# Window attention in blocks of 64 tokens, eight heads at a time, on two column tiles

## The chip, the cores and the metric

The kernel runs on one core of a Trainium2 chip. The time is device microseconds of one execution; the kernel before has a median of 1505.85 us over three runs (1504.56 to 1506.03). One more execution was profiled: 1506.56 us, of which its span in the profile is 1504.9 us. All durations below are from that execution.

## The reference

The input x holds 16 sequences ("batches" below) of 512 tokens with 128 channels. Two sublayers follow each other, each with a residual: attention in a window, and then a product-key mixture of experts. Only the first is touched here:

```python
def attn(x, w_qkv, w_proj):              # x: layer-normalised, 16 x 512 x 128
    q, k, v = split(x @ w_qkv.T)         # 16 heads of 8 channels
    s = q @ k.T / sqrt(8)                # per head, 512 x 512
    s = where(abs(i - j) > 128, -1e9, s) # a band of 128 tokens to either side
    return (softmax(s) @ v).reshape(...) @ w_proj.T
x = x + attn(layernorm(x))
x = x + experts(layernorm(x))
```

The second sublayer normalises over the whole batch of tokens, so it starts when attention is done with all 16 sequences.

## The kernel before, in words

**Units.** Attention runs over units of four heads of one sequence: 16 sequences times 4 groups, 64 units. Each unit has four steps, one for each block of 128 tokens. One pass of the loop over `s` is one step; `divmod(s, NQ)` gives unit and block.

**Operands.** `prepare(b)` normalises a sequence, transposes it, multiplies it by the weights and cuts q and k into three bf16 pieces each (on POOL), so that a sum of bf16 products has fp32 accuracy. The pieces go to DRAM (`write`), and `lay(n)` brings those of one unit back into `qst` and `kst` with six DMAs, the pieces stacked on the partition axis; a seventh DMA zeroes the three rows of `qst` from row 96. There are six buffers of each. All these DMAs stand in the queue of SP.

**Two products of the same operands.** `greatest(n, t)` multiplies the queries of one block by the keys of its neighbours (256 keys in an outer block, 384 in an inner one), four heads, into `s_ps`. DVE adds the band mask and takes the greatest of each row in one instruction (line 424). When the unit's four steps are done, `greatest_pieces` cuts the negated maxima into three bf16 pieces (five POOL operations), and `greatest_rows` transposes them on PE (`mT_ps`), copies them on ACT and sends them by DMA into the three rows of `qst`, where the matching rows of `kst` are ones. So the second product, `exponentials(n, u)` into `e_ps` with keys as rows and queries as columns, comes out with the maxima subtracted; ACT takes the exponential into `pT` (line 466). POOL then sets what is outside the band to zero with `affine_select` (through the helper at line 172), one 128 x 128 block for each neighbour, for four heads in one instruction.

**Weighing.** `weigh(n, u)` multiplies the fp32 `pT` by the values: four heads at once, each on a column tile of 32 of TensorE, summed over the steps in one PSUM bank (`o_ps`). `vaug` holds the values and a column of ones, which gives the sum for the division. `divide` transposes a unit's result (`t_ps`) and divides on DVE; `project(b)` transposes and projects a whole sequence.

**Order.** PE, through `mm` and `tr`, and POOL, through `pool`, keep the order of the program. One step emits on PE: s, e, e, s, the o products of two steps earlier (`LATE`), s, e, e, s, and then at most one block that needs the one bank of `ps_m`: `mT_ps`, `t_ps`, or the next piece of `preparing`, `ending` or `beside`. The maxima run `AHEAD` = 2 units before the exponentials, and `lay` runs four units before, at block 2. Three PSUM banks each serve `s_ps` and `e_ps`.

Of the kernel before, what the change touches and what calls it, by code (L numbers as in the profile page):

```python
# [10 lines left out]
F32 = mybir.dt.float32  # L11
# [32 lines left out]
def kernel(  # L44
# [18 lines left out]
    NG = NH // 4  # L63
# [42 lines left out]
    band_f = const.tile([P, 3, P], F32, name="band_f")  # L106
    nc.gpsimd.memset(band_f, 0.0)
    for i, sign in ((0, 1), (2, -1)):
        nc.gpsimd.affine_select(
            out=band_f[:, i], in_=band_f[:, i], compare_op=ALU.is_ge, fill=-MASKED,  # L110
            base=0, pattern=[[sign, P]], channel_multiplier=-sign,
        )
    band = const.tile([P, 3, P], BF16, name="band")
# [39 lines left out]
    with ExitStack() as at:  # L153
# [3 lines left out]
        w3 = at.enter_context(tc.tile_pool(name="w3", bufs=3))  # L157
        dr = at.enter_context(tc.tile_pool(name="dr", bufs=2, space=bass.MemoryType.DRAM))
# [21 lines left out]
        tr(wt_ps[:, 3 * P :], w_proj_sb, ident)  # L180
        for c, w in enumerate((wqT, wkT, wvT, wprojT)):
            wt = wt_ps[:, c * P : (c + 1) * P]
            if c < 2:

                w, wt = w.rearrange("p (d h) -> p d h", d=DK), wt.rearrange("p (h d) -> p d h", d=DK)
            nc.vector.tensor_copy(w, wt)
# [67 lines left out]
        vaug = [fix.tile([P, NQ, NH, VW], F32, name=f"vaug_{i}") for i in range(3)]  # L254
# [5 lines left out]
        zeros = fix.tile([P, T], BF16, name="zeros")  # L260
        nc.gpsimd.memset(zeros, 0.0)

        masked = [fix.tile([P, 3 * P], BF16, name=f"masked_{i}") for i in range(4)]

        NU, NBUF = B * NG, 6
        qst = [fix.tile([P, 4, T], BF16, name=f"qst_{i}") for i in range(NBUF)]
        kst = [fix.tile([P, 4, T], BF16, name=f"kst_{i}") for i in range(NBUF)]
# [71 lines left out]
        def prepare(b):  # L339

            xnT = w2.tile([P, T], F32, tag="xnT", name=f"xnT_{b}")
# [32 lines left out]
            if b < 3:  # L374
                nc.gpsimd.memset(va, 0.0)
                nc.gpsimd.memset(va[:, :, :, DK : DK + 1], 1.0)
            v_ps = ps_m.tile([P, NQ, NH, DK], F32, tag="m", name=f"v_ps_{b}")
            for t in range(NQ):
                mm(
                    v_ps[:, t].rearrange("p h k -> p (h k)"),  # L380
                    lhsT=xnT[:, t * P : (t + 1) * P], rhs=wvT, start=True, stop=True,
                )
            nc.scalar.copy(va[:, :, :, 0:DK], v_ps)
# [4 lines left out]
        def lay(n):  # L388
# [4 lines left out]
            for what, st in (("q", qst[n % NBUF]), ("k", kst[n % NBUF])):  # L393
                src = pieced[what, b].rearrange("s (d h) t -> s d h t", d=DK)
                for i in range(3):
                    side = src[i if what == "q" else slice(0, 3)]
                    if what == "q":
                        side = bc(side, 0, 3)
                    nc.sync.dma_start(
                        st[3 * i * DK : 3 * i * DK + 3 * DK], side[:, :, 4 * g : 4 * g + 4]  # L400
                    )

            nc.sync.dma_start(qst[n % NBUF][NR : NR + 3], bc(zeros[0:3], 1, 4))

        def near(t):

            return [u for u in (t - 1, t, t + 1) if 0 <= u < NQ]

        def greatest(n, t):

            q, k = qst[n % NBUF], kst[n % NBUF]
            if t == 0:
                tops[n] = w2.tile([P, NQ, 4], F32, tag="mx", name=f"mx_{n}")
            us = near(t)
            k0, w = us[0] * P, len(us) * P
            from_u = P if t == 0 else 0
            for h in range(4):
                s_ps = ps_s.tile([P, 3, P], F32, tag="s", name=f"s_ps_{n}_{t}_{h}")
                s = s_ps.rearrange("p u k -> p (u k)")[:, 0:w]
                mm(  # L420
                    s, lhsT=q[:, h, t * P : (t + 1) * P], rhs=k[:, h, k0 : k0 + w],
                    start=True, stop=True,
                )
                nc.vector.tensor_tensor_reduce(  # L424
                    masked[h][:, 0:w], s, band.rearrange("p u k -> p (u k)")[:, from_u : from_u + w],
                    1.0, LOWEST, ALU.add, ALU.max, tops[n][:, t, h : h + 1],
                )
                yield

        def greatest_pieces(n):  # L430

            top = tops.pop(n)
            mp = w2.tile([P, NQ, 3, 4], BF16, tag="mp", name=f"mp_{n}")
            rest = w2.tile([P, NQ, 4], F32, tag="mr", name=f"mr_{n}")
            pool("tensor_scalar_mul", rest, top, -1.0)
            pool("tensor_copy", mp[:, :, 0], rest)
            pool("tensor_tensor", rest, rest, mp[:, :, 0], ALU.subtract)
            pool("tensor_copy", mp[:, :, 1], rest)
            pool("tensor_tensor", mp[:, :, 2], rest, mp[:, :, 1], ALU.subtract)
            tops[n] = mp  # L440

        def greatest_rows(n):

            mp = tops.pop(n)
            mT_ps = ps_m.tile([12, NQ, P], BF16, tag="m", name=f"mT_ps_{n}")
            for t in range(NQ):
                tr(mT_ps[:, t], mp[:, t].rearrange("p s h -> p (s h)"), ident_bf)
            mT = w2.tile([12, T], BF16, tag="mT", name=f"mT_{n}")
            nc.scalar.copy(mT, mT_ps.rearrange("r t q -> r (t q)"))
            for i in range(3):  # L450
                nc.sync.dma_start(qst[n % NBUF][NR + i : NR + i + 1], mT[4 * i : 4 * i + 4])

        def exponentials(n, u):
# [3 lines left out]
            ts = near(u)  # L457
            q0, w = ts[0] * P, len(ts) * P
# [613 lines left out]
```

## Time and profile before

| | |
|---|---|
| median of 3 runs | 1505.85 us |
| profiled execution | 1506.56 us, span 1504.9 us |
| first s product / first e product | 38.18 us / 53.25 us |
| last block of attention on PE (xi of the last sequence) | starts at 710.98 us |
| share of the span busy | PE 93%, DVE 87%, ACT 81%, POOL 73% |
| maxima (DVE, line 424) | 1024, 459.1 us busy, mean 484 ns |
| exponentials (ACT, line 466) | 1024, 389.4 us busy, mean 436 ns |
| selects (POOL, line 172) | 384, 239.2 us busy, mean 639 ns |
| s products / e products (PE) | 1024 / 1024, mean 307 ns / 302 ns |
| o products (PE) | 2048 passes, mean 447 ns |
| DMA | mean 50 GB/s over the span, 179 GB/s in the first 40 us |

Attention takes a little under the first half of the span. In the views, "busy" of PE is from the start of a product to a modelled end that includes its way through the array, so products that follow each other closely overlap; how fast PE really goes is read from the distance between starts. A group of instructions is named by line, engine, operation, output and inputs, with partitions x elements; "128\*64" means 128 rows and 64 columns of the array. An fp32 product appears as two passes.

### The profile page before, as it was taken

The numbers are of one execution on the slowest core, as the hardware profiler recorded it, in microseconds if no ns is written. First come the engines' busy times: TensorE is split into PE (matmuls) and PEld (weight loads), VectorE is DVE, ScalarE is ACT, GpSimd is POOL, SyncE is SP. The second block draws the span as 40 slices with busy tenths as digits, with TensorE's granted clock in tenths as the row PEclk, the third lists the DMA queues.
The fourth block names the chain that finished last, engine by engine and source line by source line (L and its number), as shares of the span: only waits on it lengthen the run. The fifth ranks groups of instructions, "written<-read, shape, count | busy, mean of one in ns | idle before, by whom it ended". The sixth has DMA issues, their size and how long they took to land.

```text
span 1504.9 us, 48591 instructions
## 1 busy us (share of the span) xinstructions
PE 1395.0 (93%) x16880; PEld 844.1 (56%) x16880; DVE 1315.6 (87%) x7999; ACT 1212.4 (81%) x2596; POOL 1094.5 (73%) x1706
## 2 busy tenths in 40 slices
PE   3999999999999999896789999999999999999997
PEld 1445555544545545443456666666666666666666
DVE  6878888878888887882899999999999999999984
ACT  1577777777777777775889999999999999999963
POOL 8466666777777767563577887788878788788775
PEclk9999999999999999997999999999999999999989
DMA  6233332223333222320000000000000000000000
GB/s 177 86 111 101 102 94 84 85 79 89 92 91 92 86 85 76 101 63 36 10 9 10 9 17 10 16 17 9 16 10 17 17 10 16 10 16 10 10 2 24
DMA packets 53574, 74.96 MB, mean 50 GB/s; under 512 B 5840, under 2 KB 39888, under 8 KB 53200
## 3 DMA queue, kind: packets, MB, share of 16 engines
q1 hardware_dynamic: 52496, 71.59, 16.2%
q8 instruction: 134, 2.20, 0.6%
q14 instruction: 112, 0.92, 0.2%
q10 hardware_dynamic: 832, 0.26, 0.1%
HBM read 49.28 MB, written 20.97 MB: 47 GB/s over the span
## 4 chain that ended last, share of the span: by engine, by line
DVE 47%; PE 3%; issue 1%; ACT 1%; POOL 0%; ACTq 0%; POOLq 0%
DVE idx L624 10%; DVE row L624 9%; DVE place L624 6%; DVE top L624 6%; DVE mine L624 5%; DVE best L624 4%; DVE x_ps L624 3%; DVE num L624 2%; DVE upper L624 1%; PE up_ps L624 1%; DVE zs L624 1%; PE w_ps L624 1%; POOL cols L624 0%; PE dn_ps L624 0%; PE off_ps L624 0%
## 5 line engine op out<-in xcount | busy, mean ns | idle before, releaser
L424 DVE CUSTOM_DVE_ANT_0 masked<-s_ps,band 128x384 bf16<-128x384 f32 (+1 forms) x1024 | 459.1, 484 | 112.2 <-PE s_ps L168 95.7
L466 ACT ACTIVATE pT<-e_ps 128x384 f32<-128x384 f32 (+1 forms) x1024 | 389.4, 436 | 117.5 <-PE e_ps L168 111.1
L172 POOL TENSOR_SCALAR_AFFINE_SELECT pT<-pT 128x512 f32<-128x512 f32 x384 | 239.2, 639 | 188.8 <-ACT pT L466 187.2
L168 PE MATMUL s_ps<-kst,qst 128*128 128x384 bf16 (+1 forms) x1024 | 309.5, 307 | 22.2 <-DMA kst<-kv 11.0
L624 POOL TENSOR_TENSOR cols<-mine,wT 64x512 f32<-64x512 bf16 x256 | 270.0, 1055 | 25.7 <-ACT row L624 7.0
L624 PE MATMUL w_ps<-cols,row 128*64 128x32 f32 x8192 | 260.0, 224 | 13.6 <-POOL cols L624 13.6
L624 PEld LDWEIGHTS w_ps<-cols,row 128*64 128x64 f32 x8192 | 252.1, 139 | 32.3 <-POOL cols L624 27.8
L168 PE MATMUL e_ps<-qst,kst 128*128 128x384 bf16 (+1 forms) x1024 | 228.7, 302 | 13.1 <-ACT pT L466 12.4
L624 POOL TENSOR_TENSOR g<-g,gel 128x512 f32<-128x512 f32 x128 | 163.6, 1278 | 105.5 <-ACT g L624 105.5
L168 PEld LDWEIGHTS <-qst 128*128 128x128 bf16 x1024 | 100.5, 98 | 196.2 <-issue 168.4
L168 PE MATMUL o_ps<-pT,vaug 128*32 128x384 f32 (+1 forms) x2048 | 192.3, 447 | 0.4 <-POOL pT L172 0.4
L624 DVE FIND_INDEX8 idx<-top,sim 128x8 uint32<-128x32 f32 x1024 | 166.2, 185 | 0.0
L624 ACT ACTIVATE row<-off_p,one 128x512 f32<-128x512 bf16 x256 | 165.8, 749 | 0.0
L624 ACT ACT_TABLE_LOAD x122 | 156.5, 1283 | 2.2
L624 DVE TENSOR_TENSOR row<-x_ps,nums_p 128x1024 f32<-128x1024 f32 x128 | 150.0, 1213 | 0.0
L624 PE MATMUL up_ps<-g,key_out_sb 64*128 64x256 f32 (+2 forms) x1152 | 148.0, 384 | 0.0
L624 ACT ACTIVATE off_p<-off_ps 128x512 bf16<-128x512 f32 x256 | 132.4, 602 | 17.0 <-PE off_ps L624 16.8
L624 PE MATMUL dn_ps<-xt,key_inT 128*64 128x256 f32 x1024 | 125.6, 388 | 2.2 <-ACT sim L624 1.4
L168 PEld LDWEIGHTS <-kst 128*128 128x128 bf16 x1024 | 99.9, 98 | 45.4 <-issue 23.9
L624 PE MATMUL off_ps<-p_bf,ident_bf 128*128 128x512 bf16 x256 | 96.6, 377 | 19.7 <-ACT p_bf L624 19.6
L624 PEld LDWEIGHTS dn_ps<-xt,key_inT 128*64 128x64 f32 x1024 | 68.3, 137 | 78.3 <-ACT row L624 41.7
L624 DVE MAX8 top<-sim 128x8 f32<-128x32 f32 x1024 | 106.7, 177 | 2.9 <-ACT sim L624 2.9
(145 smaller groups left out, 2366.5 us busy)
## 6 DMA issues: line engine op xcount, KB each, us to landing
qst<-qv SPq DMA_DIRECT2D x192, 96.0 KB
kst<-kv SPq DMA_DIRECT2D x192, 96.0 KB
qv<-qp SPq DMA_DIRECT2D x16, 384.0 KB
kv<-kp SPq DMA_DIRECT2D x16, 384.0 KB
x<-in_L_attn_x_dram SPq DMA_DIRECT2D x16, 256.0 KB
xT<-xiT SPq DMA_DIRECT2D x16, 256.0 KB
xt<-xT SPq DMA_DIRECT2D x16, 256.0 KB
out_dram<-o_sb SPq DMA_DIRECT2D x16, 256.0 KB
```

The source lines that it names most:

```text
L168: tc.keep_in_program_order(nc.tensor.matmul(*args, **kw))
L172: tc.keep_in_program_order(getattr(nc.gpsimd, op)(*args, **kw))
L424: nc.vector.tensor_tensor_reduce(masked[h][:, 0:w], s, band.rearrange("p u k -> p (u k)")[:, from_u : from_u + w], 1.0, LOWEST, ALU.add, A ...
L466: nc.scalar.activation(pT[:, h, 0:w], e_ps[:, 0:w], AF.Exp)
L624: return lambda *args, **kw: tc.keep_in_program_order(op(*args, **kw))
```

## The change

The 64 units of four heads become 32 of eight. A block is 64 tokens, so a unit has eight steps; a step still makes four maxima and four exponentials, each now for a pair of heads `r` and `4 + r`: one head's 64 tokens lie on partitions 0 to 63, the other's on 64 to 127, each from its own product on a column tile of 64. A block sees two blocks of 64 to either side, so the products have 192, 256 or 320 columns. What lies outside the band are now corners of 64 x 64, selected for each half of the partitions by itself: two or four instructions a step.

The maxima of eight heads are transposed in one go (96 rows) and reach `qst` in two DMAs. `weigh` takes 128 rows that hold two heads: `vaug` has the first head's values in columns 0 to 15 of the upper partitions and the second's in columns 16 to 31 of the lower ones, so that one column tile of 32 makes both. The order of the heads changes with it, which the weights `wqT`, `wkT` and `wprojT` absorb at the start. v is computed on column tiles of 64 and copied in two halves. `qst` and `kst` have four buffers of twice the size; the zero rows are copied from unused rows of the same tile; `xnT`, `oT` and `aT` have one buffer in place of two. The maxima run 13 steps before the exponentials (8 before), and `lay` runs 20 steps before.

```diff
-    NG = NH // 4
+    HB = P // 2
+    NS = T // HB
+    NG = NH // 8
+    NR4 = 4
...
-    for i, sign in ((0, 1), (2, -1)):
+    for v in range(2):
+        half = band_f[v * HB : v * HB + HB]
         nc.gpsimd.affine_select(
-            out=band_f[:, i], in_=band_f[:, i], compare_op=ALU.is_ge, fill=-MASKED,
-            base=0, pattern=[[sign, P]], channel_multiplier=-sign,
+            out=half, in_=half, compare_op=ALU.is_ge, fill=-MASKED,
+            base=0, pattern=[[1, 5 * HB]], channel_multiplier=-1,
         )
...
+        w1 = at.enter_context(tc.tile_pool(name="w1", bufs=1))
...
-        tr(wt_ps[:, 3 * P :], w_proj_sb, ident)
+        w_proj_of = const.tile([P, NH // 2, 2, DK], F32, name="w_proj_of")
+        for j in range(2):
+            nc.vector.tensor_copy(
+                w_proj_of[:, :, j], w_proj_sb.rearrange("p (j a d) -> p j a d", j=2, d=DK)[:, j]
+            )
+        tr(wt_ps[:, 3 * P :], w_proj_of.rearrange("p a j d -> p (a j d)"), ident)
...
+                for g in range(NG):
+                    for j in range(2):
+                        nc.vector.tensor_copy(w[:, g, j], wt[:, g, j])
...
-        NU, NBUF = B * NG, 6
-        qst = [fix.tile([P, 4, T], BF16, name=f"qst_{i}") for i in range(NBUF)]
+        NU, NBUF = B * NG, 4
+        qst = [fix.tile([P, 8, T], BF16, name=f"qst_{i}") for i in range(NBUF)]
...
-            v_ps = ps_m.tile([P, NQ, NH, DK], F32, tag="m", name=f"v_ps_{b}")
-            for t in range(NQ):
-                mm(
-                    v_ps[:, t].rearrange("p h k -> p (h k)"),
-                    lhsT=xnT[:, t * P : (t + 1) * P], rhs=wvT, start=True, stop=True,
+            v_ps = ps_m.tile([P, NS, HB], F32, tag="m", name=f"v_ps_{b}")
+            for i in range(NS):
+                for j in range(2):
+                    mm(
+                        v_ps[j * HB : j * HB + HB, i], lhsT=xnT[:, i * HB : i * HB + HB],
+                        rhs=wvT[:, j * HB : j * HB + HB], start=True, stop=True, skip_group_check=True,
+                    )
+            for j in range(2):
+                half = slice(j * HB, j * HB + HB)
+                nc.scalar.copy(
+                    va[half, :, :, 16 * j : 16 * j + DK],
+                    v_ps[half].rearrange("p c (a k) -> p c a k", k=DK),
                 )
-            nc.scalar.copy(va[:, :, :, 0:DK], v_ps)
...
-            nc.sync.dma_start(qst[n % NBUF][NR : NR + 3], bc(zeros[0:3], 1, 4))
+            nc.sync.dma_start(qst[n % NBUF][NR : NR + 3], qst[n % NBUF][NR - 4 : NR - 1])
...
+        def greatest(n, i, r):
...
+            us = near(i)
+            k0, w = us[0] * HB, len(us) * HB
+            from_u = (us[0] - i + 2) * HB
+            s_ps = ps_s.tile([P, T], F32, tag="s", name=f"s_ps_{n}_{i}_{r}")
+            for j in range(2):
+                h = NR4 * j + r
                 mm(
-                    s, lhsT=q[:, h, t * P : (t + 1) * P], rhs=k[:, h, k0 : k0 + w],
-                    start=True, stop=True,
+                    s_ps[j * HB : j * HB + HB, 0:w], lhsT=q[:, h, i * HB : i * HB + HB],
+                    rhs=k[:, h, k0 : k0 + w], start=True, stop=True, skip_group_check=True,
                 )
...
+            rows = 3 * NR4 * NS
+            mT_ps = ps_m.tile([rows, P], BF16, tag="m", name=f"mT_ps_{n}")
+            tr(mT_ps, mp.rearrange("p s r i -> p (s r i)"), ident_bf)
+            mT = w2.tile([rows, P], BF16, tag="mT", name=f"mT_{n}")
+            nc.scalar.copy(mT, mT_ps)
+            for j in range(2):
+                nc.sync.dma_start(
+                    qst[n % NBUF][NR : NR + 3, NR4 * j : NR4 * j + NR4], mT[:, j * HB : j * HB + HB]
                 )
...
+            for j in range(2):
+                h = NR4 * j + r
                 mm(
-                    e_ps[:, 0:w], lhsT=k[:, h, u * P : (u + 1) * P], rhs=q[:, h, q0 : q0 + w],
-                    start=True, stop=True,
+                    e_ps[j * HB : j * HB + HB, 0:w], lhsT=k[:, h, i * HB : i * HB + HB],
+                    rhs=q[:, h, q0 : q0 + w], start=True, stop=True, skip_group_check=True,
                 )
...
+        def outside_band(n, i):
+
+            us = near(i)
+            for u, sign in ((i - 2, 1), (i + 2, -1)):
+                if u in us:
+                    at = (u - us[0]) * HB
+                    for j in range(2):
+                        side = probs[n, i][j * HB : j * HB + HB, :, at : at + HB]
+                        pool(
+                            "affine_select", out=side, in_=side, compare_op=ALU.is_ge, fill=0.0, base=0,
+                            pattern=[[0, NR4], [sign, HB]], channel_multiplier=-sign,
+                        )
...
-            for j in range(4):
+            for r in range(NR4):
                 mm(
-                    outs[n][32 * j : 32 * j + 32, q0 : q0 + w], lhsT=vaug[b % 3][:, u, 4 * g + j],
-                    rhs=pT[:, j, 0:w], start=u == 0, stop=u == NQ - 1, skip_group_check=True,
+                    outs[n][VW * r : VW * r + VW, q0 : q0 + w], lhsT=vaug[b % 3][:, i, NR4 * g + r],
+                    rhs=pT[:, r, 0:w], start=i == 0, stop=i == NS - 1, skip_group_check=True,
                 )
...
-        AHEAD, LAID, LATE = 2, 4, 2
+        AHEAD, LAID, LATE = 13, 20, 2
...
-            next(tops_of, None)
-            next(probs_of, None)
-            next(tops_of, None)
-            if 0 <= s - LATE < NU * NQ:
-                weigh(*divmod(s - LATE, NQ))
-            together(tops_of, probs_of)
+            for r in range(NR4):
+                steps = [(greatest, s + AHEAD, r), (exponentials, s, r)]
+                for what, at_s, r in steps if r % 2 == 0 else steps[::-1]:
+                    if 0 <= at_s < NU * NS:
+                        what(*divmod(at_s, NS), r)
+                if r == 1 and 0 <= s - LATE < NU * NS:
+                    weigh(*divmod(s - LATE, NS))
+            if 0 <= s < NU * NS:
+                outside_band(n, u)
             free = True
-            if u == 0 and 0 <= n + AHEAD - 1 < NU:
-                greatest_pieces(n + AHEAD - 1)
-            if u == 1 and 0 <= n + AHEAD - 1 < NU:
-                greatest_rows(n + AHEAD - 1)
+            m, of = divmod(s + AHEAD, NS)
+            if of == 0 and 0 < m <= NU:
+                greatest_pieces(m - 1)
+            if of == 1 and 0 < m <= NU:
+                greatest_rows(m - 1)
                 free = False
```

## The prediction

> **What bounds the kernel now.** I first read the page's 40 slices and then the windows. Attention fills the first half, up to about 700 us; the expert half after it is the same code in both kernels. The windows (columns: busy time and count of PE, weight loads, DVE, ACT, POOL, then granted clock, DMA share, GB/s) give the steady stretch of attention:
>
> ```profile
> 200.00:400.00 200.00, 194.19 (x1606) 100.56 (x1608) 163.42 (x738) 153.76 (x392) 140.87 (x275) 0.99 0.29 86
> 400.00:600.00 200.00, 192.36 (x1594) 98.27 (x1595) 167.23 (x746) 153.92 (x392) 143.12 (x278) 1.00 0.30 88
> ```
>
> A busy PE need not be a full one, so next I read the timeline of PE alone. The reader should see the starts: each product starts when the one before has streamed, not when it ends.
>
> ```profile
> 508.19 0.34 PE L168 MATMUL s_ps<-kst,qst 128*128 128x384 bf16 x1
> 508.36 0.49 PE L168 MATMUL e_ps<-qst,kst 128*128 128x384 bf16 x2
> 508.69 0.33 PE L168 MATMUL s_ps<-kst,qst 128*128 128x384 bf16 x1
> 508.94 0.64 PE L168 MATMUL o_ps<-pT,vaug 128*32 128x256 f32 x8
> 509.51 0.34 PE L168 MATMUL s_ps<-kst,qst 128*128 128x384 bf16 x1
> ```
>
> A 384-wide product takes 0.163 us (508.69 is three after 508.19, with 0.17 first), that is 384 columns at 2.4 per ns plus 3 ns. The eight 256-wide o passes start 0.25 after the last s (0.16 of it streaming, 0.09 a gap) and hold PE 0.57: 4 x 256/2.4 = 0.427, four column tiles side by side, plus 0.143. So a change from 128 columns to 32 and back costs 0.09 + 0.145 = 0.235 us.
>
> Sum for one batch (4 groups of 4 steps, widths 256, 384, 384, 256): s and e 4 x 8 x 1280/2.4 = 17.1, plus 3 ns x 128 = 0.4; o 4 x 4 x 1280/2.4 = 8.5; 16 changes 3.8; four mT blocks at 0.42 (517.53 to 517.86 and the gap before) 1.7; four t_ps at 0.43 1.7; xn 0.43, q and k 0.86 each, v 0.9, a 0.43, y 0.9, xi 0.43, together 4.8. That is 38.0 us. The stretch holds 638 maxima (64 a batch), so a batch lasts 400 x 64/638 = 40.1. What PE waits for is in the tile view of mp:
>
> ```profile
> who waited for it (us, times):
>   PEld L175: 14.5, 36
>   PE mT_ps L175: 2.4, 7
> ```
>
> 16.9 us in ten batches is 1.7 a batch; 0.4 is left. PE bounds attention, and the other engines need 33.1 (DVE), 30.8 (ACT) and 28.5 (POOL) of the 40.1.
>
> **The change, part by part, per batch** (now two groups of eight steps, widths 192, 256, 4 x 320, 256, 192: 2176 a group).
>
> *s and e.* 128 products become 128 pairs on two column tiles. Whether a pair costs one stream or two decides everything. The expert half has such pairs:
>
> ```profile
> 899.48 0.59 PE L624 MATMUL sim_ps<-wsim,xb 128*128 128x512 f32 x1
> 900.00 1.95 PE L624 MATMUL dn_ps<-xt,key_inT 128*64 128x256 f32 x16
> 906.74 0.28 PE L624 MATMUL x_ps<-ident_bf,num_bf 128*64 128x64 bf16 x6
> 908.88 0.38 PE L624 MATMUL off_ps<-less_nums,ident_bf 128*128 128x512 bf16 x1
> 909.19 0.34 PE L624 MATMUL s_ps<-ident,share 128*64 128x64 f32 x4
> 909.45 1.13 PE L624 MATMUL up_ps<-g,key_out_sb 64*128 64x256 f32 x8
> ```
>
> Sixteen dn passes of 256 fp32 columns (0.213 each by the 2 cycles a column seen in q_ps) end in 1.95: seven spacings plus one of 0.379 makes 0.22 a pair, so a pair costs one stream and its weight loads hide. Six bf16 products end in 0.28 although one takes 0.196. So a pair is width/2.4 + 3 ns: 2 x 8 x 2176/2.4 = 14.5 + 0.4. Bounds: one stream, or two (+14.5 us a batch, 1704 in all); I take one, because dn is the same tile shape.
>
> The Trainium skill, TensorEngine Tiling (Array Packing), Restrictions, says that column tiling disables the fast weight load; its page TensorE: Matmul & The Clock Gate, LDWEIGHTS, gives columns/1.2 ns. By an estimate from that, two loads of 64 take 107 ns, which exceeds only the 192-wide stream of 80: 27 ns x 32 pairs, 0.9 us a batch, 14 us in all, 1486 for 1472. No run here shows that; the x_ps row speaks against it.
>
> *o.* 4 x 2176/2.4 x 2 = 7.25; still one change per step, 3.8.
>
> *mT and t_ps.* Four transposes into one of 96 columns; half as many blocks: 2 x 0.053 and 2 x 0.43.
>
> *New changes of tiling.* s and e now stand at 64 columns, so each 128-column block (mT 2, t_ps 2, xn, q, k, a, y, xi: 10) pays a change in and out. Priced by the rows above: sim 128 to dn 64 leaves 0.52 - 0.427 = 0.09; off to s_ps 0.31 - 0.213 = 0.09; s_ps to up_ps 0.26 - 0.107 = 0.15. Again 0.235: 2.35 a batch. Bounds 0 and twice that (1434 and 1510); I take the rows. v_ps moves into the 64 mode: 16 pair passes at the 0.062 of w_ps (128 products in 3.96), 1.0 for 0.9. Other blocks unchanged, 3.9.
>
> PE sum: 14.9 + 7.25 + 3.8 + 0.1 + 0.86 + 2.35 + 1.0 + 3.9 = 34.1.
>
> *Selects on POOL.* 24 of 128x512 become 48 of 64x256.
>
> ```profile
> L172 POOL TENSOR_SCALAR_AFFINE_SELECT pT<-pT 128x512 f32<-128x512 f32 x89 | 55.6, 641 | 45.4 <-ACT pT L466 45.2
> L109 POOL TENSOR_SCALAR_AFFINE_SELECT band_f<-band_f 128x128 f32<-128x128 f32 x2 | 0.5, 294 | 0.0
> ```
>
> Between 128 and 512 elements the slope is 0.9 ns, so 256 take 0.41, or 0.385 in a row (0.27 and 0.615 for the two shapes). Half the partitions save nothing: four 64-partition cols products in a row take 4.42 (1.1 each), not side by side. Bounds 0.2 (side by side) and 0.64. 18.5 for 15.
>
> *Pieces.* Five POOL operations per group, 1.39 from first to last, twice instead of four times. POOL in all: 28.5 - 15 - 4.4 + 18.5 + 2.5 = 30.
>
> *Where the stall goes.* mT waits on PE for the pieces, and everything behind it on PE waits too. Before, the pieces followed a step with one select (0.64). Now they come at u == 3, behind four. The selects start 0.8 after the step's last s (510.01 to 510.99 less streaming), take 1.56, the pieces 1.45: ready at 3.8. PE reaches mT one 320-wide step later (8 x 0.136 + 0.533 + 0.235 = 1.86) plus 0.09, in even groups also after a_ps (0.67): stalls of 1.8 and 1.2, 3.0 a batch for 1.7. W (the o products) two steps on finds its selects done; where POOL carries 0.6 to 1.2 of query and key pieces per step it still keeps up (9.8 us against PE's 10.2 over the four wide steps).
>
> *DVE, ACT.* The maxima cost 0.345 at 256 and 0.478 at 384 in a row, so 0.28 and 0.41 at 192 and 320: 23.2 for 26.4, in all about 29. Exponentials 397 mean for 436; mT copies 2 x 0.27 for 4 x 0.56, oT 2 for 4, one more v copy of 0.59: 26. Both stay below PE. Twice eight reciprocals and products ride on DVE's spare 8 us.
>
> *DMA and SP.* The lay issues halve in number and double in size (192 KB); 0.30 of DMA is used and a group is laid seven steps, 16 us, before its first product. The mT rows go in two issues of 96 pieces of 128 bytes in place of three; three full steps, 6 us, lie between, against SP's 0.6 an issue. The zero rows come from the tile itself on the same queue: nothing. Single buffers for xnT, oT and aT: each is read within a step or two of being written and rewritten eight or more steps later: nothing.
>
> *Start.* First s at 38.18 waits for kst. The first group is now twice as large: 0.29 MB more at 179 GB/s, 1.6 us; six more small DVE copies for the weights, about 1; band, clears and vaug lie under POOL's 6.7 us wait for qf. The lead of 13 steps for 8 leaves five more steps at each end with only one kind of product: (1.45 + 1.5 - 2.35) x 5 = 3. Together +6.
>
> **Sum.** Batch: 34.1 + 3.0 + 0.4 = 37.5 for 40.1, -2.6; over 16 batches less the longer ends (243 of 256 steps) -40; with the start -34. The profiled execution took 1506.56 (span 1504.9), 0.7 above the median 1505.85: 1472.
>
> **Rivals.**
> - *POOL takes over (slower).* At POOL's share of 0.95, 11.5 + 48c = 0.95 x 40.1 is reached at c = 0.55 per select; beyond, it is slower. At the full-size row's 0.615: 41.0, period 43, +46 + 6: 1558. For: selects double in number and sit in runs of four, before the pieces that PE waits for. Against: the 128x128 row.
> - *Pairs do not share the array (slower).* From 20 ns lost a pair on (2.6/128) the gain is gone; fully serial 1704. For: these exact bf16 widths appear nowhere before. Against: dn and x_ps.
> - *The gain is larger.* Selects side by side, or changes between 64 and 128 columns free, or no mT stall (-3.0 x 16): 1424 to 1445.
> - *No change that can be measured (within 3 us, 0.2%, about what can be told here):* stalls of 5.2 us a batch in place of 3; 1506.
>
> **How the numbers follow.** Forecast 0.52 (1450 to 1495, faster). Larger gain 0.14. POOL 0.24, of it slower 0.16, same 0.04, slightly faster 0.04. Pairs or their loads exposed 0.10, slower. Faster 0.70, same 0.04, slower 0.26. The range leaves out half of the larger gain's low end and most of the pairs' case: 1440 to 1540.
>
> **What would show it.** Right: s_ps products 128*64 in twos with starts some ns apart, pairs 0.136 apart at 320; selects 64x256 near 0.41; PE still the only engine above 90% of a batch of 37 to 38 us; mT waits of 1 to 2 us for mp, 64 us in all. Wrong: the starts of a pair a full stream apart; selects near 0.6; o_ps waiting for POOL in most steps; gaps around t_ps or q_ps well off 0.235; s_ps waiting for DMA into kst or e_ps for the mT rows.

## The result and the profile after

| | before | after |
|---|---|---|
| median | 1505.2 us (4 runs) | 1590.6 us (4 runs, 1587.7 to 1593.0) |
| ratio, with its 95% interval | 1 | 1.0567 (1.0545 to 1.0588) |
| first e product | 53.2 us | 69.9 us |
| first dn product (attention is over) | 712.1 us | 795.8 us |
| one batch in the steady stretch | 40.6 us | 44.9 us |

The kernel became 5.7% slower; 1472 was forecast. All of it lies in attention: from the first dn product to the end of the span both kernels need some 793 to 795 us. The last row divides 450 us (200 to 650) by the batches in it, counted in exponentials or s products, 64 a batch.

The windows of the kernel after (columns as before: busy time and count of PE, weight loads, DVE, ACT, POOL, then granted clock, DMA share, GB/s):

```profile
200.00:400.00 200.00, 169.01 (x2003) 88.31 (x1999) 134.90 (x643) 120.89 (x337) 140.91 (x309) 0.96 0.28 76
400.00:600.00 200.00, 172.03 (x2029) 91.14 (x2029) 138.75 (x660) 119.22 (x336) 143.30 (x315) 0.94 0.28 81
```

Every engine has become idler: PE went from 97% to 85%, DVE from 83% to 68%, and POOL stands at 71% as it did. No engine is full over a stretch of 200 us, and the granted clock fell from 0.99 to 0.95. So something waits in turns. The page's groups say that the operations themselves came out as forecast or better (busy us, mean ns, then idle time before them and its releaser):

```profile
L448 DVE CUSTOM_DVE_ANT_0 masked<-s_ps,band 128x320 bf16<-128x320 f32 (+2 forms) x1024 | 413.0, 437 | 211.5 <-PE s_ps L177 205.2
L493 ACT ACTIVATE pT<-e_ps 128x320 f32<-128x320 f32 (+2 forms) x1024 | 344.6, 398 | 171.7 <-PE e_ps L177 166.0
L181 POOL TENSOR_SCALAR_AFFINE_SELECT pT<-pT 64x256 f32<-64x256 f32 x768 | 317.3, 413 | 200.3 <-ACT pT L493 173.6
```

Selects take 413 ns, against 0.41 us in the forecast. The timeline of PE shows where it stands still (start, duration or extent, then in brackets the idle time before it and the releaser):

```profile
503.22 0.36 PE L177 MATMUL s_ps<-kst,qst 128*64 128x192 bf16 x4
503.41 0.70 PE L177 MATMUL e_ps<-qst,kst 128*64 128x320 bf16 x4
503.92 0.30 PE L177 MATMUL s_ps<-kst,qst 128*64 128x256 bf16 x2
504.15 0.75 PE L177 MATMUL o_ps<-pT,vaug 128*32 128x320 f32 x8
504.82 0.30 PE L177 MATMUL s_ps<-kst,qst 128*64 128x256 bf16 x2
504.96 0.44 PE L177 MATMUL e_ps<-qst,kst 128*64 128x320 bf16 x4
505.23 0.28 PE L177 MATMUL s_ps<-kst,qst 128*64 128x256 bf16 x2
508.03 0.26 PE L184 MATMUL mT_ps<-ident_bf,mp 128*96 128x128 bf16 x1 [2.52 <-POOL mp L181]
508.21 0.33 PE L177 MATMUL s_ps<-kst,qst 128*64 128x320 bf16 x2
508.38 0.44 PE L177 MATMUL e_ps<-qst,kst 128*64 128x320 bf16 x4
508.65 0.30 PE L177 MATMUL s_ps<-kst,qst 128*64 128x320 bf16 x2
```

Two things are to be seen. Two pairs of 320-wide e products take from 508.38 to 508.65, 0.136 a pair: a pair costs one stream, as forecast. And in front of `mT_ps` PE stands still for 2.5 us, waiting for the last of the pieces on POOL. On POOL the same moment reads:

```profile
501.92 1.79 POOL L181 TENSOR_SCALAR_AFFINE_SELECT pT<-pT 64x256 f32<-64x256 f32 x4 [0.98 <-ACT pT L493]
503.81 0.81 POOL L181 TENSOR_SCALAR xn<-x,mva,rsa 128x128 f32<-128x128 f32 x1
504.58 1.79 POOL L181 TENSOR_SCALAR_AFFINE_SELECT pT<-pT 64x256 f32<-64x256 f32 x4
506.46 0.30 POOL L181 TENSOR_SCALAR mr<-mx 128x32 f32<-128x32 f32 x1
506.83 0.21 POOL L181 CAST mp<-mr 128x32 bf16<-128x32 f32 x1
507.13 0.25 POOL L181 TENSOR_TENSOR mr<-mr,mp 128x32 f32<-128x32 f32 x1
507.44 0.21 POOL L181 CAST mp<-mr 128x32 bf16<-128x32 f32 x1
507.73 0.24 POOL L181 TENSOR_TENSOR mp<-mr,mp 128x32 bf16<-128x32 f32 x1
```

From 501.92 on POOL has no pause: four selects, a block of the next sequence's normalisation, four selects, five operations for the pieces. The tile view of `mp` for 200 to 650 us adds these waits up (us, times):

```profile
who waited for it (us, times):
  PEld L184: 54.2, 20
  PE mT_ps L184: 48.3, 20
  ACT mT L472: 43.3, 20
```

Twenty waits, one for each group of eight heads, 48.3 us: 4.8 a batch, where 3.0 was forecast.

The clock is the second thing. Windows around one of these waits (the first ends where PE stops, the second is the wait):

```profile
544.70:548.10 3.40, 3.33 (x48) 1.62 (x44) 2.85 (x15) 2.19 (x6) 3.08 (x7) 1.00 0.02 5
548.10:551.10 3.00, 0.48 (x7) 0.19 (x5) 0.69 (x4) 0.77 (x2) 2.51 (x9) 1.00 0.00 0
551.10:554.50 3.40, 3.40 (x24) 1.20 (x24) 1.50 (x6) 1.30 (x4) 2.09 (x5) 0.50 0.05 7
554.50:557.90 3.40, 3.40 (x32) 1.60 (x30) 2.96 (x12) 2.30 (x7) 1.86 (x5) 1.00 0.56 135
```

After the wait PE looks fully busy for 3.4 us, but at half the clock. Between 200 and 650 us the clock was halved for 51 us, fifteen times 3.41 us, in 13 spells of which two are of double length; before, there were two spells of 3.41 us. Eleven of the twenty waits for `mp` had such a spell within 2 us.

The start is the third. First s and first e products by tile (count, then ns and the time of the first and the last in the window), after:

```profile
L177 PE MATMUL s_ps<-kst,qst x784: 242/299/476, 47.2 to 299.6; 128*64 128x320 bf16 x96, 128*64 128x192 bf16 x50, 128*64 128x256 bf16 x50
```

```profile
L177 PE MATMUL e_ps<-qst,kst x680: 242/297/474, 69.9 to 299.4; 128*64 128x320 bf16 x86, 128*64 128x192 bf16 x42, 128*64 128x256 bf16 x42
```

Nine us more to the first s, 16.6 more to the first e.

To add up a batch I read the distances between the starts of PE's products. What a product needs to stream, at full clock, goes to "stream"; the 0.235 for going from one tiling to another to "changes"; the excess where the clock is halved to "clock"; what is left over is idle, put down to the product that it precedes. This counts more idle time than the views of waits do, since those measure from the modelled end of a product, some 0.2 us after its stream. It is my reading of the trace; the parts fall some 0.6 us short of the batch.

| us a batch | stream | changes | clock | idle | of it before mT | e_ps | s_ps | o_ps |
|---|---|---|---|---|---|---|---|---|
| before, 40.6 | 32.6 | 4.1 | 0.3 | 3.0 | 0.3 | 1.2 | 1.0 | 0.4 |
| after, 44.9 | 27.3 | 5.4 | 2.1 | 9.5 | 4.9 | 2.7 | 0.7 | 0.5 |

The change does what it says, 5.3 us less streaming a batch for 1.3 more changes of tiling; then 6.5 us of new waits and 1.8 of clock take more than that back.

### The profile page after: what moved, and what is told of

Read it like the earlier page. It is cut to its first block, busy times and chain, and to the rows that moved or that the text cites. A ratio compares the mean times of both kernels' runs of the same rounds, so it can differ in the third digit from the quotient of the medians.

```text
span 1590.4 us, 53099 instructions
## 1 busy us (share of the span) xinstructions
PE 1394.9 (88%) x18960; PEld 852.3 (54%) x18960; DVE 1271.7 (80%) x7943; ACT 1150.3 (72%) x2548; POOL 1149.5 (72%) x1930
## 4 chain that ended last, share of the span: by engine, by line
DVE 48%; PE 28%; POOL 13%; ACT 5%; issue 4%; DMA 1%; SPq 0%; ACTq 0%; POOLq 0%; DVEq 0%
DVE idx L656 10%; DVE row L656 9%; PE s_ps L177 7%; POOL pT L181 7%; PE o_ps L177 6%; DVE place L656 6%; DVE top L656 5%; PE e_ps L177 5%; DVE mine L656 4%; DVE best L656 4%; ACT pT L493 3%; DVE x_ps L656 2%; DVE num L656 2%; PE y_ps L177 1%; POOL mp L181 1%
## 5 line engine op out<-in xcount | busy, mean ns | idle before, releaser
L448 DVE CUSTOM_DVE_ANT_0 masked<-s_ps,band 128x320 bf16<-128x320 f32 (+2 forms) x1024 | 413.0, 437 | 211.5 <-PE s_ps L177 205.2
L493 ACT ACTIVATE pT<-e_ps 128x320 f32<-128x320 f32 (+2 forms) x1024 | 344.6, 398 | 171.7 <-PE e_ps L177 166.0
L181 POOL TENSOR_SCALAR_AFFINE_SELECT pT<-pT 64x256 f32<-64x256 f32 x768 | 317.3, 413 | 200.3 <-ACT pT L493 173.6
L177 PE MATMUL s_ps<-kst,qst 128*64 128x320 bf16 (+2 forms) x2048 | 302.0, 304 | 28.1 <-DMA kst<-kv 19.2
L177 PE MATMUL e_ps<-qst,kst 128*64 128x320 bf16 (+2 forms) x2048 | 233.0, 295 | 22.6 <-ACT pT L493 21.6
L177 PEld LDWEIGHTS <-qst 128*64 128x64 bf16 x2048 | 124.8, 113 | 200.3 <-issue 187.3
L177 PE MATMUL o_ps<-pT,vaug 128*32 128x320 f32 (+2 forms) x2048 | 180.9, 427 | 1.5 <-POOL pT L181 1.5
L177 PEld LDWEIGHTS <-kst 128*64 128x64 bf16 x2048 | 124.4, 114 | 53.2 <-issue 43.9
```

Of the source, the lines that this page charges most:

```text
L177: tc.keep_in_program_order(nc.tensor.matmul(*args, **kw))
L181: tc.keep_in_program_order(getattr(nc.gpsimd, op)(*args, **kw))
L448: nc.vector.tensor_tensor_reduce(masked[r][:, 0:w], s_ps[:, 0:w], band[:, from_u : from_u + w], 1.0, LOWEST, ALU.add, ALU.max, tops[n][:, ...
L493: nc.scalar.activation(probs[n, i][:, r, 0:w], e_ps[:, 0:w], AF.Exp)
```

## The experiments

The theory after this reading: POOL is behind in the stretch of four-select steps (blocks with two neighbours on either side, products 320 wide; called wide steps below), and the pieces, which stand behind those selects, hold PE up. Its rivals: that the place of the wait in PE's order is to blame (a later mT would find the pieces ready); that it is the step distance between maxima and exponentials; and that part of the loss is the clock and not POOL's time. The ratios below are to the kernel before, run on the same chip.

### The rows one step later

```diff
-            if of == 1 and 0 < m <= NU:
+            if of == 2 and 0 < m <= NU:
                 greatest_rows
```

> Only the transposition of the maxima's pieces (mT_ps) moves, by one step (from the second step after a group's last maximum to the third). Theory (PE waits at mT_ps for POOL's pieces, 5.0 us a batch in the changed kernel, and its clock is halved after such waits, 1.9 us a batch): the wait of about 2.5 us per group shrinks by one step, some 1.9 us, so 3.8 us a batch, and most of the 1.9 us of the clock goes too; over 15 batches about 80 us, 1510 us. Rival (POOL's 768 selects bound attention, the wait at mT_ps is only where this shows): the wait comes back at o_ps or mT_ps, 1580 to 1595 us.

Measured: 1579.1 us, 1.0485 (1.0467 to 1.0502); 44.0 us a batch. The waits of PE by the profile (total us, times, longest), 200 to 650:

```profile
PE xn_ps L184 <- POOL xn L181: 28.9, 10, 3.5
PE o_ps L177 <- POOL pT L181: 18.4, 20, 2.2
PE e_ps L177 <- ACT pT L493: 12.3, 27, 3.2
...
PE mT_ps L184 <- POOL mp L181: 0.2, 1, 0.2
```

The wait for `mp` is gone, from 48.3 to 0.2, and 47.3 us of waits for other results of POOL stand in its place. So the place of mT isn't the cause: POOL is late with all that it makes in that stretch. The time is near the rival's 1580 us, not the 1510 of the theory.

### The pieces ahead of the selects

```diff
+            m, of = divmod(s + AHEAD, NS)
+            if of == 0 and 0 < m <= NU:
+                greatest_pieces(m - 1)
             if 0 <= s < NU * NS:
                 outside_band(n, u)
             free = True
-            m, of = divmod(s + AHEAD, NS)
-            if of == 0 and 0 < m <= NU:
-                greatest_pieces(m - 1)
```

> Only POOL's order changes: the five operations that cut the maxima into pieces stand before the four selects of their step, not behind them. Theory (the pieces come late because of the 1.8 us of selects ahead of them): the wait at mT_ps falls from 2.5 us to under 0.7 us per group, the selects of that step come 1.5 us later, for which the o products two steps on have room; 60 to 90 us less, 1500 to 1530 us. Rival (POOL's load bounds): what mT_ps no longer waits, o_ps waits; 1580 to 1595 us.

Measured: 1542.2 us, 1.0245 (1.0218 to 1.0273); 42.1 a batch. PE's waits:

```profile
PE o_ps L177 <- POOL pT L181: 20.8, 31, 0.8
PE mT_ps L184 <- POOL mp L181: 12.9, 19, 1.8
```

With the pieces first, 48 us of the gap of 85 are gone. What is left changes place again: the selects come later, and now the o products wait for them in 31 steps. The order of POOL's work made a good half of the loss. That its amount is still too much is argued from the new waits here and tested below.

### More distance between maxima and exponentials

```diff
-        AHEAD, LAID, LATE = 13, 20, 2
+        AHEAD, LAID, LATE = 16, 22, 2
```

> The maxima run 16 steps (two whole groups) before the exponentials and not 13, and the operands are laid 22 steps before and not 20. Two things follow: the pieces stand behind a step with two selects, not four, as in the kernel before; and the s and e products of a step have the same width, so no step has wide exponentials with narrow maxima. Theory (wait at mT_ps 5.0, clock 1.9, and e_ps waiting for a free bank 2.4 us a batch through the unequal widths): a batch of about 36 to 37 us, that is 7.5 us x 15.5 less, three more steps of lead cost some 3 us: 1470 to 1480 us, below the kernel before. If unequal widths cost nothing: about 1500 us. Rival (POOL's load bounds): 1580 us or more.

Measured: 1563.4 us, 1.0362 (1.0319 to 1.0405); 42.5 a batch, the wait for mT 3.1 for 4.9, and the first e product at 82.1 us for 69.9. This lead puts the pieces behind a step with two selects in place of four. It saves 2.4 us a batch and pays 12 us at the start. Both the theory (1470 to 1480 us) and the rival missed: the waits got shorter, but most of them stayed.

### The wait filled with products that nobody reads

```diff
+            fill = ps_m.tile([P, 5 * HB], F32, tag="m", name=f"fill_{n}")
+            for _ in range(16):
+                mm(fill, lhsT=ident_bf, rhs=band, start=True, stop=True)
             mT_ps = ps_m.tile([rows, P], BF16, tag="m", name=f"mT_ps_{n}")
```

> Sixteen products of 128x320 bf16 (0.136 us each, 2.2 us) that nothing reads stand on PE just before each transposition of the pieces, where PE waits about 2.5 us for POOL. The wait of everything else stays; only PE is no longer idle in it. Theory (the idle time itself lowers the granted clock, and this costs 1.9 us a batch beyond the wait): the granted clock in attention goes from 0.95 to 0.99 or more and 25 to 30 us are saved, 1560 to 1565 us. Rival (the low clock falls into time that PE has to spare anyway): 1585 to 1600 us, with the filling adding up to 0.3 us per group where the wait was shorter.

Measured: 1564.9 us, 1.0392 (1.0373 to 1.0412); 42.9 a batch. The window 200 to 650:

```profile
200.00:650.00 450.00, 428.30 (x5036) 233.93 (x5037) 317.23 (x1517) 282.84 (x788) 333.92 (x732) 0.99 0.28 81
```

PE does 4.3 us more a batch, and the kernel is 26 us faster than with the wait left empty. POOL's work and the order are the same; what moved is the clock. It is back at 0.99, two halved spells of 3.41 us are left of the fifteen, and of the 2.0 us that a batch gains 1.8 are the clock's in my account. The wait costs twice: once while it lasts and once after it.

### One select for both halves

The lower half gets the corner of the upper: half of the selecting is left out, so the output is another.

```diff
-                    for j in range(2):
-                        side = probs[n, i][j * HB : j * HB + HB, :, at : at + HB]
+                    side = probs[n, i][:, :, at : at + HB]
```

> The two selects of a side (64 partitions each) become one over all 128 partitions, so a wide step has two selects in place of four and POOL has 384 selects of 128x256 in place of 768 of 64x256. The corner of the lower 64 partitions is then selected wrongly: this leaves out half of POOL's selecting and nothing else. Theory, as it stands after the first four runs (POOL is behind only in the wide steps: 4 selects 1.8 us and 0.6 to 1.6 us of other work against a step of PE of some 2.1 us; PE then stands at whatever next needs POOL, at mT_ps, xn_ps or o_ps): without 0.9 us a wide step POOL keeps up, the waits at mT_ps fall from 5.0 to about 1 us a batch, the clock comes back (1.9), a batch is 37 to 38 us: 1475 to 1490 us. Rival (the waits come from the order of the work and the unequal widths alone, whatever POOL's load): 1560 us or more.

Measured: 1510.1 us, 1.0034 (1.0021 to 1.0047); 39.9 a batch. The window 200 to 650:

```profile
200.00:650.00 450.00, 409.04 (x5063) 218.43 (x5062) 345.06 (x1649) 304.30 (x849) 239.47 (x512) 0.99 0.33 91
```

Half of the selects away brings 80 of the 85 us back, the clock included. That settles the cause, POOL's selects; that they hurt in the wide steps is read from the timelines. The ten runs spread from 1503.9 to 1513.9 us, and the profiled one is the shortest. The 1475 to 1490 us expected were missed: what stays is a wait for `mp` of 1.7 a batch and 2.6 before e products. The steady stretch is now quicker than in the kernel before (39.9 for 40.6), but the first e product still comes at 70.1 us, 16.9 later, and that takes the gain back.

### The corners masked on PE

The band tile is multiplied by the identity and added to `e_ps`, so ACT's exponential comes out as zero there; POOL selects nothing.

```diff
+            for u in (i - 2, i + 2):
+                if u in us:
+                    at, of = (u - us[0]) * HB, (u - i + 2) * HB
+                    for j in range(2):
+                        mm(
+                            e_ps[j * HB : j * HB + HB, at : at + HB], lhsT=ident_bf[:, 0:HB],
+                            rhs=band[:, of : of + HB], start=False, stop=True, skip_group_check=True,
+                        )
...
-                outside_band(n, u)
```

> No selects at all: the corners outside the band are pushed to -1e9 in PSUM before the exponential, by one more product of the identity (64 columns) with 64 columns of the band mask, accumulated on the e product for each corner and head. POOL loses 768 x 0.41 us; PE gains 1536 products of 64 columns, in pairs of 0.03 to 0.06 us, 1.4 to 2.9 us a batch. Theory (POOL in the wide steps): mT_ps waits under 1 us a batch, o_ps no longer waits for POOL, the clock stays full; batch 32.7 + 2.2 + about 3 of e_ps and s_ps waits = 38: 1475 to 1490 us, below the kernel before. Rival (narrow pairs and their changes of tiling cost PE more than the trace shows): not under 1540 us, since PE only gets more to do.

Measured: 1510.6 us, 1.0037 (1.0023 to 1.0051); 39.8 a batch. The added products on PE:

```profile
440.98 0.23 PE L177 MATMUL e_ps<-band,ident_bf 128*64 128x64 bf16 x4
441.04 0.31 PE L177 MATMUL e_ps<-qst,kst 128*64 128x320 bf16 x2
```

Four of them, for one pair of heads, hold PE for 0.06 us (440.98 to 441.04): 0.24 in a wide step for four selects of 1.79 together, and at this price 2.9 for the 192 products of a batch (3072 in all; the 1536 expected are pairs), for the 20 us (48 x 0.413) of POOL's time that they replace. The wait for mT is nil, and what is left idle is 3.7 a batch, of it 2.3 before e products. The batch missed the expected 38 by 1.8, and the time by 20 us; the late start is as in the run before.

### The same with a lead of 16

```diff
-                outside_band(n, u)
...
-        AHEAD, LAID, LATE = 13, 20, 2
+        AHEAD, LAID, LATE = 16, 22, 2
```

(and the products of the mask, as above)

> As the run with the mask on PE, and the maxima 16 steps ahead in place of 13, so that the s and e products of a step have the same width. Theory (unequal widths make ACT late in steps of wide e and narrow s, and DVE late in the opposite steps; 2.5 us a batch of waiting at e_ps): 1 to 1.5 us a batch less than the same kernel with 13, 15 to 20 us, less 3 to 5 us for the longer lead. Rival (e_ps waits come from blocks such as t_ps and q_ps that bunch ACT's work, not from the widths): the same time within 5 us, or a little slower by the lead.

Both edits together gave 1517.0 us, 1.0082 (1.0065 to 1.0099): 39.5 a batch for 39.8, and the first e product at 81.3 for 70.1. The lead also changes which widths of s and e meet in a step; the waits before e hardly moved (2.1 for 2.3). The longer start outweighs it.

### One corner on PE, one on POOL

The mask of the sixth experiment for `i - 2` only, a select for `i + 2` only, and the pieces first.

```diff
+            for u in (i - 2,):
+                if u in us:
...
-            for u, sign in ((i - 2, 1), (i + 2, -1)):
+            for u, sign in ((i + 2, -1),):
```

> The earlier corner of each step is masked on PE (half of the added products of the run with the whole mask on PE), the later one stays a select on POOL, and the pieces stand before the selects. Theory (POOL's four selects in a run of wide steps were the cause; two are borne): mT_ps waits 0.3 to 0.8 us a batch; PE streams 1.3 us a batch less than with the whole mask on PE, so a batch of 38.6 to 39.2 us and 1490 to 1500 us, below the kernel before. Rival (any select ahead of the o products stalls PE): o_ps waits 1 us a batch or more, 1510 us or more.

Measured: 1501.5 us, 0.9971 (0.9957 to 0.9984); 39.3 a batch. POOL at the place of a wide run:

```profile
506.89 0.88 POOL L181 TENSOR_SCALAR_AFFINE_SELECT pT<-pT 64x256 f32<-64x256 f32 x2
507.84 0.61 POOL L181 CAST qp<-rest_q 128x512 bf16<-128x512 f32 x1
508.57 0.89 POOL L181 TENSOR_SCALAR_AFFINE_SELECT pT<-pT 64x256 f32<-64x256 f32 x2
509.54 1.16 POOL L181 TENSOR_TENSOR qp<-rest_q,qp 128x512 bf16<-128x512 f32 x1
510.67 0.30 POOL L181 TENSOR_SCALAR mr<-mx 128x32 f32<-128x32 f32 x1
```

Two selects and one piece of the next sequence in a step, and the pieces no longer wait behind selects. This version is 0.3% faster than the kernel before, with an interval that stays just below 1: the narrow products do gain, 40.6 to 39.3 a batch, when POOL is relieved.

### A PSUM bank from s to e

```diff
-        ps_s = at.enter_context(tc.tile_pool(name="ps_s", bufs=3, space=PSUM))
-        ps_e = at.enter_context(tc.tile_pool(name="ps_e", bufs=3, space=PSUM))
+        ps_s = at.enter_context(tc.tile_pool(name="ps_s", bufs=2, space=PSUM))
+        ps_e = at.enter_context(tc.tile_pool(name="ps_e", bufs=4, space=PSUM))
```

(on the kernel with all corners on PE)

> The whole mask on PE, and one PSUM bank moved from the s products (3 to 2) to the e products (3 to 4). Theory (what is left, 2.3 us a batch at e_ps, is PE finding no free bank where two steps follow each other without a block between them and so two pairs of e products meet): e_ps falls to about 1 us a batch, s_ps rises by 0.3 to 1: 0 to 15 us less than with three banks each, 1495 to 1511 us. Rival (ACT itself is late there, and the bank only shows it): e_ps stays above 2 us and s_ps rises: 1515 to 1530 us.

Measured: 1522.7 us, 1.0114 (1.0094 to 1.0133). The waits before e fell from 2.3 to 1.2 a batch and those before s rose from 0.3 to 2.1: a batch takes 40.3 us for 39.8. The larger part of the 12 us is lost at the start, where the first e product comes at 78.9 us for 70.1. The banks are not to spare on either side.

### A lead of 12

The shared mask with one step less between maxima and exponentials.

```diff
-        AHEAD, LAID, LATE = 13, 20, 2
+        AHEAD, LAID, LATE = 12, 19, 2
```

> As the run with the shared mask, with the maxima 12 steps ahead in place of 13 and the operands laid 19 ahead in place of 20. Theory (the longer lead at the start costs, about 1.5 to 3.5 us a step by the first e product at 70 us against 82 us with 16 steps): 1.5 to 4 us less than the same kernel with 13. Rival (the time between the rows' DMA and the first exponential, now some two steps, is too short): e_ps waits for the rows in each group, 0.5 us or more, 10 us or more slower.

Measured: 1559.9 us, 1.0358 (1.0329 to 1.0387); 43.6 a batch. PE's waits, 200 to 600:

```profile
PE e_ps L177 <- DMA qst<-mT: 34.2, 9, 4.5
```

One step less, and in nine of the eighteen groups the e products wait for the rows of the maxima, up to 4.5 us, with the clock down to 0.94 again. They are the nine groups in which the last transfer of a `lay` was issued 3.5 to 4.0 us before the rows: there the rows' packets were through 6.0 to 8.0 us after their issue, while some 0.85 to 1.15 MB of other packets moved. In the other nine they were through after 2.5 us, and nothing waited. So 12 steps are enough for the rows alone; what they lack is room for the `lay` ahead of them, which with 13 steps was issued 4.9 us before the rows or earlier. A lead of 12 with the `lay` at another place was not run.

### The same order of s and e in each half step

```diff
-                for what, at_s, r in steps if r % 2 == 0 else steps[::-1]:
+                for what, at_s, r in steps:
```

(on the shared mask)

> As the run with the shared mask, with the products of a step in the order s, e, s, e on either side of the o products in place of s, e, e, s. Theory (2.7 us a batch of waiting at e_ps arise where two steps follow each other without a block between them and four e products start within 0.7 us, against 0.4 us an exponential and three banks; now they start within 0.8 us): e_ps waits 0.5 to 1 us a batch less, 5 to 15 us, 1487 to 1497 us. Rival (ACT is late for other reasons, its copies): within 4 us of 1501.

Measured: 1497.8 us, 0.9955 (0.9940 to 0.9970); 39.1 a batch, the waits before e 1.9 for 2.7, those before s 1.2 for 0.5. This is the lowest time of all, 0.45% below the kernel before; its interval meets that of the shared mask (0.9957 to 0.9984), so the step between the two is not certain. That two pairs of e stood next to each other (e, e in "s e e s") thus explains some of the waits before e, not all.

The main runs side by side; all columns but the median are of the one profiled execution of each, whose time stands second, and "clock" to "e_ps" are us a batch by the account above.

| | median us | profiled us | a batch | clock | idle | before mT | e_ps | first e |
|---|---|---|---|---|---|---|---|---|
| after | 1590.6 | 1592.1 | 44.9 | 2.1 | 9.5 | 4.9 | 2.7 | 69.9 |
| rows later | 1579.1 | 1573.8 | 44.0 | 1.5 | 9.3 | 0.0 | 2.8 | 73.0 |
| wait filled | 1564.9 | 1565.7 | 42.9 | 0.3 | 4.9 | 0.6 | 2.6 | 71.5 |
| lead 16 | 1563.4 | 1562.8 | 42.5 | 1.0 | 8.1 | 3.1 | 2.4 | 82.1 |
| pieces first | 1542.2 | 1540.4 | 42.1 | 0.6 | 8.2 | 1.3 | 2.5 | 72.2 |
| one select a side | 1510.1 | 1503.9 | 39.9 | 0.3 | 6.5 | 1.7 | 2.6 | 70.1 |
| corners on PE | 1510.6 | 1510.6 | 39.8 | 0.1 | 3.7 | 0.0 | 2.3 | 70.1 |
| shared mask | 1501.5 | 1498.7 | 39.3 | 0.3 | 4.7 | 0.1 | 2.7 | 69.7 |

## Why the prediction was wrong

The time lies above the range, and the sign is wrong. The batch was forecast at 37.5 us and took 44.9, 7.4 more. By the account above: stream and changes -1.4 (32.7 for 34.1), mT +1.9 (4.9 for 3.0), the clock +2.1, other idle time +4.2 (4.6 for 0.4), and the 0.6 that the account doesn't place.

- **Right: the PE sum.** Pairs share the array (0.136 a pair at 320), the changes of tiling cost what the rows said, weight loads show nowhere. The rival "Pairs do not share the array" is out, and so is the price put on what the Trainium skill says of weight loads in column tiling (TensorEngine Tiling (Array Packing), Restrictions): two 192-wide pairs of e products held PE from 513.92 to 514.08, 0.08 each, which is their stream, so no load showed.

```profile
513.92 0.33 PE L177 MATMUL e_ps<-qst,kst 128*64 128x192 bf16 x4
514.08 0.30 PE L177 MATMUL s_ps<-kst,qst 128*64 128x320 bf16 x2
```

- **Right: the price of a select**, 413 ns for 0.41, and the loads of DVE and ACT, which fell.
- **Wrong: "Where the stall goes".** This is the step that failed. In the timeline above, the selects began 1.3 after the step's last s where 0.8 was forecast, because `xn` of the next sequence stood ahead of them; four took 1.79 and not 1.56 ((1.79 - 0.413)/3 = 0.46 from start to start, where the forecast had 0.385); the pieces 1.6 and not 1.45. Ready at 4.7, not 3.8. And the clause that POOL "still keeps up", 9.8 us against 10.2, was the judgement that all hung on. It left 0.4 us of slack in four steps, with prices known to no better than that. With 1.79 for selects and 0.6 to 1.2 for the next sequence's work a step needs 2.4 to 3.0 on POOL, against 2.55 on PE by that same clause; where a piece of 1.16 stands between them, the fours of selects were in fact 2.99 apart (481.34 and 484.33, 488.24 and 491.23).
- **Wrong: the break-even of the rival "POOL takes over".** It asked from which price of a select POOL would be 95% busy over a batch, 0.55. The selects cost 0.41, POOL is 70% busy, and yet it decides, because its work isn't spread evenly: four selects a step in the run of inner blocks, two at the ends, and PE can't run ahead of it by more than a step or two. The right sum would have been over one wide step. That rival's 1558 was nearer to the result than the forecast, though not by its own mechanism.
- **Missing: the clock.** No term of the sum and no rival spoke of it, though the stalls forecast were of 1.2 to 1.8 us and the trace before had two halved spells. It cost 2.1 us a batch, and the experiment with the filled wait gave 26 us back. By the reading in the last section, waits of 1.2 to 1.8 would seldom have brought it on; those of 2.5 often did. The Trainium skill, TensorE: Matmul & The Clock Gate, Why this matters for your kernels, advises against idle gaps of PE over some 3 us. Here less was enough: only two of the twenty waits were over 3 us, and one of 1.63 too was followed by a halved spell.
- **Wrong: "0.4 is left".** The time before was put down as 38.0 for PE and 1.7 for mT. By the distances of the starts PE needed 36.7, and the 1.7 was almost all the weight load's wait, during which the products before it still streamed: the product itself lost 0.3. So 2.7 us of waits before e, s and o products lay in terms of the sum that were booked too high, and nothing in the forecast said what would become of them. They grew to 4.6, the part before e from 1.2 to 2.7. The even order of s and e takes 0.8 of that back and gives 0.7 to the waits before s; the rest stays open.
- **Too small: the start.** +6 was forecast for both ends; the first e product alone came 16.6 us later, of the 83.7 by which attention ends later. One wait holds the first s (waits of PE, 0 to 72 us):

```profile
PE s_ps L177 <- DMA kst<-kv: 17.2, 1, 17.2
```

From the write of the key pieces (`kv<-kp`, issued at 31.18, before at 28.07) to the first s product 16.0 us pass for 10.1, with 179 GB/s moved in these first 40 us; the 13 steps to the first e product take 22.7 for 15.1. The forecast had 1.6 for the bytes and 3 for the lead at both ends. The write itself comes 3.1 later, 2.2 of it already at the first cast of q's pieces on POOL (17.19 for 14.97). This is read from the traces; no run tested it.
- **The sign that the prediction named,** "o_ps waiting for POOL in most steps", did not show in the kernel after: there mT caught all of the lateness, and o_ps waited only once mT was moved away.

## What to carry to other kernels

Where two engines keep the order of the program and a few buffers lie between them, compare their work step by step in the heaviest run of steps, not over the whole period: an engine at 70% can hold up another at 97%. A wait on PE can have a second price, half the clock for 3.4 us after it, so a stall of about 2 us or more should be booked at more than its length. And a select that is split to fit half the partitions costs its full price twice (413 ns on 64 partitions, 418 on 128); look for the engine on which such work is cheap (here 0.24 us a wide step on PE for 1.79 on POOL).

## What was not expected of the hardware

- After waits of 1.6 to 3.7 us PE's granted clock was 0.50 for 3.41 us, once for twice that, in 11 of 20 cases. The length of the wait does not decide: 1.63 did at 346 us, 2.52 at 508 us did not. But all spells of a run begin whole multiples of 3.413 us apart, and if one cuts the time into windows at these places, it is seen what does. Two waits of 2.52 (from 505.50 and from 548.32) in such windows, columns as before:

```profile
503.31:506.72 3.41, 2.13 (x28) 0.87 (x24) 2.16 (x12) 2.17 (x6) 3.07 (x7) 1.00 0.01 2
506.72:510.13 3.41, 2.10 (x25) 1.01 (x25) 1.12 (x5) 1.10 (x4) 2.97 (x10) 1.00 0.01 2
547.68:551.10 3.42, 0.90 (x15) 0.51 (x13) 0.81 (x4) 0.77 (x2) 2.89 (x10) 1.00 0.02 5
551.10:554.51 3.41, 3.41 (x24) 1.20 (x24) 1.50 (x6) 1.31 (x4) 2.09 (x5) 0.50 0.05 7
```

The first wait falls on two windows, with PE idle for 1.3 us in each, and the clock stays. The second lies in one window, and the next has half the clock. In the traces of all 13 kernels, 200 to 650 us, of the windows at full clock every one with PE idle for 1.84 us or more was followed by half the clock (41 of 41), none with less than 1.62 was (0 of 1568), and 13 of the 21 between.
- A select of 64 x 256 elements takes 413 ns, and one of 128 x 256, in the run with one select a side, 418: half the partitions save nothing. On the two halves in turn the selects of a row start 0.46 apart, so two on different halves do not overlap at all, and are spaced wider than one lasts; two of 128 x 256 in a row take 0.79, so they start 0.37 apart.
- PE can be made faster by giving it more to do: 16 useless products a group, 4.3 us a batch, made the kernel 26 us shorter.
